# A four-layer graph network on one core: the products of layer 0 a batch later, four rows' sums ahead of the last two, and later small steps in layer 1

## The chip, the cores and the metric

The kernel runs on one core of a Trainium2 chip. The metric is device time in microseconds (us) of the whole kernel. The core has five engines that issue their instructions in order, each on its own: TensorE (PE, matmuls and transpositions), VectorE (DVE), ScalarE (ACT), GpSimd (POOL) and SyncE (SP, which here starts most DMA transfers). Matmuls accumulate in PSUM[...]; the rest is in SBUF, and large matrices are in DRAM.

## The reference

A graph has N = 3125 nodes with 128 features, and 103,125 edges: 50,000 random pairs in both directions, and a loop on each node. Four layers follow each other.

```python
# layer 0: weighted sum over the edges, bias, relu; then layer norm of x + out
xw  = x @ weight
out = relu(segment_sum(edge_weight[:, None] * xw[src], dst) + b)
# layer 1: attention with 4 heads of 32
e     = leaky_relu(a_s[src] + a_d[dst])
p     = exp(e - segment_max(e, dst)[dst])
alpha = p / (segment_sum(p, dst)[dst] + 1e-16)
out   = segment_sum(h[src] * alpha[:, :, None], dst) + gat_bias + x @ skip_W + skip_b
# then a layer norm of its own, and another one around x + out
# layer 2: attention with Q, K, V over the same edges, softmax per receiver
# layer 3: two products with the mean over the neighbours (w1_l, w1_r, b1, w2_l, w2_r, b2)
```

## The kernel before, in words

The nodes make 25 blocks of 128. Sums over edges are done as matmuls with dense block matrices. Two of these are built first, in DRAM: `wd`, the summed weights of the edges between each two blocks, and `ctd` (`f_ctd` in the trace), their counts.

**Edge stage** (from L841). The edges, sorted, are cut into windows; 40 batches of 16 windows. For a batch DVE makes two one-hot masks (`ohd`, `ohc`, L865) and their products with the weights in three bf16 parts (`wod`, L876; the last part in halves with ACT, L882). `make(b + 1)` runs while PE works on batch b. For each four windows PE does 8 matmuls `cp` (counts, L911) and 24 `wp` (weights, L919), and ACT copies both out of PSUM (`cs` L924, `ws` L930). SP stores `ws` to `wd` after each batch (L941), and `cs` to `ctd` after each second one.

**Layer 0** runs inside that. Row i of `wd` is complete some batches before the end. Then `adds0` issues on SP the loads of the row's 20 blocks (two tiles `cw` of 640 KB, pool `f_zp` of four buffers) and puts 20 products (L820, two passes each) on the list `todo`. After each four windows up to three of the list are issued on PE. The program writes the order of PE and SP out by hand in this stage (`manual_schedule`); on DVE and ACT a scheduler orders.

```python
            if order:
                m = min(3, len(todo)) if b > 3 else 0
                for f in todo[:m]:
                    f()
                del todo[:m]
                if len(todo) <= 20 and (done + 1) * P <= (b - 1) * BW * WN:
                    todo += adds0(zp, done, acc0, (0, Z0))
                    done += 1
```

The sums for blocks 0 to 19 (`acc0`) take five PSUM banks, so blocks 20 to 24 (`acc1`) can't be summed in the same stage. After the last batch comes the **tail**: what is left of `todo`, and the last rows of `acc0`. Then `front.close()` frees the memory of the edge stage, and the **left rows** follow: all 25 rows once more for blocks 20 to 24, five products a row, loads of 320 KB in a pool of eight buffers (`f_tp1`). Beside them run the end of layer 0 (`end0`: relu, add, layer norm; `r` L832), the attention scores of layer 1 (`scores1`, `top`, `factors`), hung on rows by `marks`, and `values`, which makes layer 1's `vp` for two blocks at a time.

**Layer 1** loops over items (g, hp, c): four groups g of 6, 7, 6 and 6 destination blocks, two pairs of heads hp, and 25 source blocks c. A half pass is one (g, hp). `masks` loads counts (`ct1`) and makes a mask `cm` for each head, two of five in one DVE instruction (L1280), the others on ACT (`fm` L1286) and DVE (L1287). `products` does three matmuls a block (L1297, L1302 twice). At c = 24 `sums` adds up on DVE (`nz` L1321), and POOL and DVE divide. Small work is put between the items: `later(k, f)` hands f to the k-th `step()` from now, and there is one step an item. After a group's second half `finish1` runs: norm, scale, multiply and add on POOL, norm, scale, and then `turns`: the blocks of the group one by one are transposed (L1044), multiplied (L1048) and copied to `vo` (L1050, `self__8043` in the trace), in the one or two PSUM banks that `few` gives (two only where the group has under seven blocks). `skips` (L1310, L1311) starts the next group's sum for the residual.

**Layer 2** loops over two halves q of the destination blocks (13 and 12) and 25 source blocks c: scores L1445 on PE, exponential L1448 on ACT, counts L1449 on DVE, products L1453. `degrees` prepares the division of layer 3 (`rt` L1425). **Layer 3** is two passes (L1553, L1629).

## Time and profile before

| | |
|---|---|
| median of 3 runs | 1505.42 us (1503.63 to 1510.78) |
| the profiled execution | 1509.73 us |
| its span, as the profile has it | 1507.9 us |
| PE busy, PEld (weight loads) busy | 1394.0, 1225.2 us |
| DVE, ACT, POOL busy | 981.9, 908.5, 129.5 us |
| mean granted clock of PE | 0.974 |
| edges end (last wp) | 463.3 us |
| last product of blocks 0 to 19 | 488.6 us |
| left rows | 494.5 to 537.2 us |
| half passes of layer 1 start their `nz` at | 596.4, 638.7, 699.0, 749.9, 806.4, 851.6, 905.3, 946.2 us |

The profile is that of one execution. Its page cuts the span in 40 slices and gives for each the busy share of every engine in tenths, the granted clock of PE (PEclk) in tenths of full speed, and the share of the DMA engines. A row of PE's timeline has start, length, engine, line, operation, output and inputs by the program's names, and in brackets the idle time just before it and what ended that. A row of the chain of waits has start, length and what took it. Half passes are cut here at the start of `nz`: what PE does in 638.7 to 699.0 is the half pass (1, 0), and so on.

### The profile page before, as it was taken

The numbers are of one execution on the slowest core, as the hardware profiler recorded it, in microseconds if no ns is written. First come the engines' busy times: TensorE is split into PE (matmuls) and PEld (weight loads), VectorE is DVE, ScalarE is ACT, GpSimd is POOL, SyncE is SP. The second block draws the span as 40 slices with busy tenths as digits, with TensorE's granted clock in tenths as the row PEclk, the third lists the DMA queues.
The fourth block names the chain that finished last, engine by engine and source line by source line (L and its number), as shares of the span: only waits on it lengthen the run. The fifth ranks groups of instructions, "written<-read, shape, count | busy, mean of one in ns | idle before, by whom it ended". The sixth has DMA issues, their size and how long they took to land.

```text
span 1507.9 us, 35015 instructions
## 1 busy us (share of the span) xinstructions
PE 1394.0 (92%) x14762; PEld 1225.2 (81%) x14775; DVE 981.9 (65%) x1621; ACT 908.5 (60%) x1857; POOL 129.5 (9%) x164
## 2 busy tenths in 40 slices
PE   3889999999998988988979989899999999999995
PEld 3889999999998877987978989677777774458995
DVE  4989899999991389887888879544464351012006
ACT  2978789888882489877777787454465331023003
POOL 1000000000000023132032113200000000000000
PEclk8999999999999999999999999999999999999998
DMA  7378788989887733433534534332222218513641
GB/s 206 94 184 229 194 221 241 236 212 229 240 213 223 230 115 114 138 106 107 142 83 116 143 86 116 124 112 69 69 64 77 81 58 299 198 43 131 199 154 46
DMA packets 209732, 223.91 MB, mean 148 GB/s; under 512 B 72988, under 2 KB 183371, under 8 KB 209309
## 3 DMA queue, kind: packets, MB, share of 16 engines
q1 hardware_dynamic: 208780, 218.51, 50.5%
q8 instruction: 117, 1.92, 0.5%
q0 software_dynamic: 400, 1.97, 0.4%
q10 hardware_dynamic: 385, 1.11, 0.2%
q14 instruction: 50, 0.41, 0.1%
HBM read 157.19 MB, written 64.36 MB: 147 GB/s over the span
## 4 chain that ended last, share of the span: by engine, by line
PE 72%; DVE 10%; ACT 8%; DMA 5%; issue 3%; POOL 2%; SPq 0%; DVEq 0%; ACTq 0%; POOLq 0%
PE wp L919 11%; PE acc L1453 9%; PE acc L1302 9%; PE s L1445 8%; PE acc L1553 7%; PE acc L1629 6%; PE acc L820 6%; PE acc L1297 5%; PE cp L911 4%; DVE cm L1287 3%; ACT wod L882 3%; DMA cw<-wd 2%; PE left L820 2%; ACT fm L1286 1%; DVE cm L1280 1%
## 5 line engine op out<-in xcount | busy, mean ns | idle before, releaser
L1302 PE MATMUL acc<-vp,cm 128*128 128x198 bf16 x2500 | 343.3, 252 | 7.6 <-DVE cm L1287 6.5
L1297 PE MATMUL acc<-vp,ct 128*128 128x204 bf16 x1250 | 316.5, 255 | 10.2 <-DVE vp L1205 4.5
L1286 ACT ACTIVATE fm<-adr,bas 128x768 bf16<-128x768 f32 (+1 forms) x320 | 287.2, 952 | 62.2 <-DVE cm L1287 60.4
L1302 PEld LDWEIGHTS <-cm 128*128 128x128 bf16 x2500 | 235.7, 98 | 24.4 <-DVE cm L1287 8.8
L919 PE MATMUL wp<-wod,ohc 128*128 128x128 bf16 x3768 | 239.1, 220 | 6.8 <-ACT cs L924 5.0
L919 PEld LDWEIGHTS <-ohc 128*128 128x128 bf16 x3768 | 220.3, 98 | 8.3 <-issue 7.8
L876 DVE TENSOR_TENSOR wod<-ohd,w 128x4096 bf16<-128x4096 bf16 (+2 forms) x122 | 221.5, 1869 | 0.4 <-PE wp L919 0.4
L1287 DVE TENSOR_TENSOR cm<-fm,ct 128x768 bf16<-128x768 bf16 (+1 forms) x320 | 200.3, 657 | 32.1 <-PE acc L1302 16.3
L882 ACT ACTIVATE wod<-ohd,wu 128x128 bf16<-128x128 bf16 x628 | 197.9, 398 | 0.0
L1449 DVE TENSOR_TENSOR e<-e,ct 128x416 f32<-128x416 f32 (+1 forms) x175 | 108.1, 624 | 110.2 <-ACT e L1448 102.1
L1448 ACT ACTIVATE e<-s,f_nm 128x416 f32<-128x416 f32 (+1 forms) x175 | 109.5, 632 | 103.1 <-PE s L1445 95.5
L1453 PEld LDWEIGHTS acc<-self__8043,e 128*128 128x128 f32 x1250 | 148.2, 193 | 19.8 <-issue 18.9
L820 PE MATMUL acc<-f_xw,cw 128*128 128x128 f32 x1000 | 146.8, 288 | 11.1 <-DMA cw<-wd 11.1
L1453 PE MATMUL acc<-self__8043,e 128*128 128x129 f32 x1250 | 148.5, 276 | 0.0
L1445 PE MATMUL s<-yT,f_xT 128*128 128x416 f32 (+1 forms) x350 | 143.1, 545 | 4.5 <-ACT rt L1425 2.5
L820 PEld LDWEIGHTS acc<-f_xw,cw 128*128 128x128 f32 x1000 | 126.5, 196 | 11.8 <-DMA cw<-wd 11.8
L1297 PEld LDWEIGHTS <-ct 128*128 128x128 bf16 x1250 | 121.8, 98 | 4.1 <-issue 2.9
L924 ACT CAST cs<-cp 128x500 bf16<-128x500 f32 x157 | 90.6, 577 | 39.1 <-PE cp L911 39.1
L1445 PEld LDWEIGHTS s<-yT,f_xT 128*128 128x128 f32 x350 | 62.6, 192 | 55.3 <-issue 40.8
L865 DVE TENSOR_TENSOR ohd<-kd,ramp 128x4096 bf16<-128x4096 bf16 (+1 forms) x41 | 90.2, 2201 | 20.2 <-PE cp L911 18.3
L930 ACT COPY ws<-wp 128x512 f32<-128x512 f32 x157 | 90.1, 578 | 20.6 <-PE wp L919 20.3
L911 PE MATMUL cp<-ohc,ohd 128*128 128x125 bf16 x1256 | 96.0, 220 | 4.1 <-ACT ws L930 3.8
(345 smaller groups left out, 1526.3 us busy)
## 6 DMA issues: line engine op xcount, KB each, us to landing
ct<-f_ctd SPq DMA_DIRECT2D x46, 800.0 KB
wd<-ws SPq DMA_DIRECT2D x39, 896.0 KB
cw<-wd SPq DMA_DIRECT2D x50, 640.0 KB
ct<-f_ctd SPq DMA_DIRECT2D x150, 192.0 KB
f_ctd<-cs SPq DMA_DIRECT2D x20, 1000.0 KB
ct<-f_ctd SPq DMA_DIRECT2D x50, 224.0 KB
ct<-f_ctd SPq DMA_DIRECT2D x25, 416.0 KB
ct<-f_ctd SPq DMA_DIRECT2D x25, 365.2 KB
```

Source lines behind the costliest of these rows:

```text
L820: steps.append(lambda j=j, a=cw[:, j - h, :]: nc.tensor.matmul(accs[j // 4][:, j % 4, :], a, xw[:, i, :], start=False, stop=(i == NB - 1 a ...
L876: tip[s] = nc.vector.tensor_tensor(packed(f, ww), packed(ohd, ww), twos(w2[s])[:, ww], OP.mult)
L882: nc.scalar.activation(wod[2][:, BW + w, :], ohd[:, BW + w, :], AF.Copy, scale=w3[:, 1, at : at + 1])
L911: nc.tensor.matmul(cp[:, j, 0:KW], ohd[:, w, :], ohc[:, w, 0:KW], start=(j == 0 and q == 0), stop=(j == 3 and q == 1), skip_group_check=True,)
L919: made = nc.tensor.matmul(wp[:, j, :], ohc[:, w, :], wod[s][:, w, :], start=(j == 0 and q == 0 and s == 0), stop=(j == 3 and q == 1 and s ...
L1286: nc.scalar.activation(f[:, : n * P], at, AF.Relu, bias=bas[:, c, h : h + 1], scale=UP)
L1287: nc.vector.tensor_tensor(m[:, : n * P], f[:, : n * P], ct[:, : n * P], OP.min)
L1297: nc.tensor.matmul(out_(F1, PW), ct[:, k * P : (k + 1) * P], vp[:, c, hp : hp + 2, :, 2 * F1 : V1], start=(c == 0), stop=False, skip_group ...
L1302: nc.tensor.matmul(out_(0, 2 * F1)[:, j], ms[j][:, k * P : (k + 1) * P], vp[:, c, hp + j, :, 0 : 2 * F1], start=False, stop=(c == NB - 1 a ...
L1445: nc.tensor.matmul(s[:, :m], xT[:, c * P : (c + 1) * P], yT[:, i0 * P + a : i0 * P + a + m], start=True, stop=True)
L1448: nc.scalar.activation(e[:, a : a + m], s[:, :m], AF.Exp, bias=nm[:, q : q + 1], scale=scale)
L1453: nc.tensor.matmul(acc[k // 3][:, (k % 3) * (P + 1) : (k % 3 + 1) * (P + 1)], es[q, c][:, k * P : (k + 1) * P], vo[:, c, 0 : P + 1], start ...
```

## The change

It has these parts:

- The products from `todo` start at batch 5 instead of 4: twelve of them move behind the last batch.
- After the last batch the three PSUM banks of the edge stage are closed at once (`three`), and the banks of blocks 20 to 24 are opened in the tail with their bias. After row 22 come rows 0 to 3 for blocks 20 to 24 (ZA = 4), in the same four buffers, and then rows 23 and 24 for blocks 0 to 19. By the order of the program row 22's loads, which were issued in the last but one batch, now stand in the tail behind the last stores.
- The pools for counts (`f_cp1`) and for one factor of the masks (`f_dp1`) are opened ahead of the pool of the left rows, so in memory of their own; the pool of the masks stays in the memory of the left rows.
- The left loop starts at row 4. Its marks move on by four rows; `values` stand after rows 16, 18, 19, 21, 22 and 24 instead of every odd row from 13.
- The masks of the first two items are emitted ahead of `end0` of blocks 20 to 24.
- `norm1` loses its square root, which becomes a step of its own (`root`), a gap later; `finish1`'s gaps go from (1, 5) to (2, 9), for the last group from (1, 1) to (1, 2); `turns` start four steps after the second scale instead of one; `bound2` of the first half waits three steps, and three more.
- `skips` start at c = 5 instead of 2, and `degrees` at c = 16 instead of 3; `finish2` has the root as a step too.

```diff
@@ -495,6 +495,7 @@
 NBT = NW // BW
 LW = 4
 NL = (NBT - 1) * BW + LW
+ZA = 4
 Z0 = 20
 V1 = 100
 GA = 80.0
@@ -570,7 +571,8 @@
     op_ = front.enter_context(tc.tile_pool(name="f_oh", bufs=2))
     of_ = front.enter_context(tc.tile_pool(name="f_of", bufs=6))
     ep = front.enter_context(tc.tile_pool(name="f_ep", bufs=1))
-    cps = front.enter_context(tc.tile_pool(name="f_cps", bufs=3, space=PSUM))
+    three = ctx.enter_context(ExitStack())
+    cps = three.enter_context(tc.tile_pool(name="f_cps", bufs=3, space=PSUM))
     ramp = ep.tile([P, P], BF16, name="ramp")
     thr = ep.tile([P, NG], F32, name="thr")
     row_i = ep.tile([P, NG], I32, name="row_i")
@@ -929,7 +931,7 @@
                 cur[3](k)
             nc.scalar.copy(ws[:, k : k + 4, :], wp)
             if order:
-                m = min(3, len(todo)) if b > 3 else 0
+                m = min(3, len(todo)) if b > 4 else 0
                 for f in todo[:m]:
                     f()
                 del todo[:m]
@@ -955,9 +957,21 @@
             order = ExitStack()
             order.enter_context(tc.manual_schedule(engines={mybir.EngineType.PE, mybir.EngineType.SP}))
     order.close()
+    three.close()
+    zpp = zero.enter_context(tc.tile_pool(name="f_zpp", bufs=1, space=PSUM))
+    left = GB[Z0 // 4 :]
+    acc1 = [zpp.tile([P, 4, P], F32, name=f"left{k}") for k in range(len(left))]
+    t8 = zpp.tile([P, 512], F32, name="tr_sa")
+    for a, (b0, n) in zip(acc1, left):
+        bias0(a, n)
     for f in todo:
         f()
-    for i in range(done, NB):
+
+    for i in range(done, NB - 2):
+        add0(zp, i, acc0, (0, Z0))
+    for i in range(ZA):
+        add0(zp, i, acc1, (Z0, NB - Z0))
+    for i in range(max(done, NB - 2), NB):
         add0(zp, i, acc0, (0, Z0))
     front.close()
     r = xw
@@ -1023,8 +1037,10 @@
             nc.vector.bn_aggr(mv[:, b, :], bs[:, b, :])
         sd = sp.tile([P, 13], F32, name="sd1")[:, 0:n]
         nc.vector.tensor_scalar(sd, mv[:, :, 1], EPS, None, OP.add)
-        nc.scalar.activation(sd, sd, AF.Sqrt)
         return sp, mv, sd
+
+    def root(state):
+        nc.scalar.activation(state[2], state[2], AF.Sqrt)
     def norm2(state, o, i, i0, n):
         sp, mv, sd = state
@@ -1056,15 +1072,22 @@
         i0, n = QG[q]
         mq = sp.tile([P, 1], F32, name="mq")
         nc.vector.tensor_reduce(mq, nq[:, i0 : i0 + n], AX.X, OP.max)
-        d = highest(sp, mq, 1)
-
-        def rest():
+        wait = 1 if q else 3
+
+        def rest(d):
             mm = sp.tile([P, 1], F32, name="mm")
             spread(d, 1, mm)
             nc.scalar.activation(mm, mm, AF.Sqrt)
             nc.vector.tensor_scalar(nm[:, q : q + 1], mm, -1.0001, None, OP.mult)
-        later(1, rest)
+        def over():
+            d = highest(sp, mq, 1)
+            later(wait, lambda: rest(d))
+
+        if q:
+            over()
+        else:
+            later(wait, over)
     def finish1(sp, g, gap):
@@ -1075,7 +1098,8 @@
         def first_norm():
             keep["a"] = norm1(sp, r, i0, n)
-            later(gap[0], first_scale)
+            later(gap[0], lambda: root(keep["a"]))
+            later(gap[0] + 1, first_scale)
         def first_scale():
             norm2(keep["a"], r, r, i0, n)
@@ -1086,12 +1110,13 @@
         def second_norm():
             keep["b"] = norm1(sp, r, i0, n)
-            later(gap[0], second_scale)
+            later(gap[0], lambda: root(keep["b"]))
+            later(gap[0] + 1, second_scale)
         def second_scale():
             norm2(keep["b"], x, r, i0, n)
             nc.gpsimd.memset(vo[:, i0 : i0 + n, P : P + 1], 1.0)
-            later(gap[0], lambda: turns(0))
+            later(1 if g == len(IG) - 1 else 4, lambda: turns(0))
         def turns(j):
             if j < n:
@@ -1126,14 +1151,10 @@
         HW = 3 * PW
         fp = st.enter_context(tc.tile_pool(name="f_fp1", bufs=2))
+        cp = st.enter_context(tc.tile_pool(name="f_cp1", bufs=6))
+        dp = st.enter_context(tc.tile_pool(name="f_dp1", bufs=2))
         tail = ExitStack()
         tp = tail.enter_context(tc.tile_pool(name="f_tp1", bufs=8))
-        zpp = zero.enter_context(tc.tile_pool(name="f_zpp", bufs=1, space=PSUM))
-        left = GB[Z0 // 4 :]
-        acc1 = [zpp.tile([P, 4, P], F32, name=f"left{k}") for k in range(len(left))]
-        t8 = zpp.tile([P, 512], F32, name="tr_sa")
-        for a, (b0, n) in zip(acc1, left):
-            bias0(a, n)
         for g in range(Z0 // 4):
             end0(acc0[g], *GB[g])
@@ -1207,7 +1228,7 @@
                 )
         spare.append(lambda: zps.tile([P, 512], F32, name="few", tag="acc1"))
-        marks = {3: lambda: scores1(0), 4: lambda: (scores1(1), scores1(2)), 5: lambda: scores1(3), 6: lambda: scores1(4)}
+        marks = {7: lambda: scores1(0), 8: lambda: (scores1(1), scores1(2)), 9: lambda: scores1(3), 10: lambda: scores1(4)}
         keep = {}
         def top():
@@ -1216,23 +1237,19 @@
             nc.vector.tensor_reduce(ex, sa[:, 0:Z0, 0:H].rearrange("p b h -> p h b"), AX.X, OP.max)
             keep["d"] = highest(fp, ex, H)
-        marks[7] = top
-        marks[9] = lambda: (spread(keep["d"], H, km), factors(0, Z0))
+        marks[11] = top
+        marks[13] = lambda: (spread(keep["d"], H, km), factors(0, Z0))
         ready = 0
-        for i in range(NB):
+        for i in range(ZA, NB):
             add0(tp, i, acc1, (Z0, NB - Z0))
             if i in marks:
                 marks[i]()
-            if i >= 13 and i % 2:
+            if i >= 16 and i % 3 != 2:
                 values(ready)
                 ready += 2
         tail.close()
-        cp = st.enter_context(tc.tile_pool(name="f_cp1", bufs=6))
         mp = st.enter_context(tc.tile_pool(name="f_mp1", bufs=8))
-        dp = st.enter_context(tc.tile_pool(name="f_dp1", bufs=2))
         sp = st.enter_context(tc.tile_pool(name="f_sp1", bufs=2))
-        for g, (b0, n) in enumerate(left):
-            end0(acc1[g], b0, n)
         later(3, lambda: scores1(Z0 // 4))
         later(5, lambda: scores1(Z0 // 4 + 1))
         later(7, lambda: factors(Z0, NB - Z0))
@@ -1342,12 +1359,16 @@
                 rh = r[:, i0 : i0 + n, hp * C : (hp + 2) * C].rearrange("p b (h c) -> p b h c", c=C)
                 nc.gpsimd.tensor_tensor(rh, rh, hi[:, :, :, 0:C], OP.add)
                 if hp == H - 2:
-                    later(1 if last else 3, lambda: finish1(ends[-1], g, (1, 1) if last else (1, 5)))
+                    later(1 if last else 3, lambda: finish1(ends[-1], g, (1, 2) if last else (2, 9)))
             later(1 if last else 4 if g else 7, quotients)
         ends.append(sp)
         acc = None
+        for y_ in range(2):
+            masks(*items[y_])
+        for g, (b0, n) in enumerate(left):
+            end0(acc1[g], b0, n)
         for x_, (g, hp, c) in enumerate(items):
             i0, n = IG[g]
             if (g, hp, c) == (1, 0, 0):
@@ -1367,7 +1388,7 @@
                     acc += [zpp.tile([P, 512], F32, name="acc1", tag=k) for k in ("tr_sa", "left0", "left1")]
                 else:
                     acc = [ap.tile([P, 512], F32, name=f"acc1_{k}") for k in range(n)]
-            if c == (2 if g else 0) and hp == (0 if g else H - 2):
+            if c == (5 if g else 0) and hp == (0 if g else H - 2):
                 later(0, lambda: skips(i0, i0 + n))
             if (g, hp, c) == (0, 2, 5):
                 later(0, in_range)
@@ -1375,7 +1396,7 @@
             if g == 0 and hp == 0 and ready < NB and ready <= c + 4:
                 values(ready)
                 ready += 2
-            for y_ in range(x_ if x_ == 0 else x_ + 2, min(x_ + 3, len(items))):
+            for y_ in range(x_ + 2, min(x_ + 3, len(items))):
                 masks(*items[y_])
             if c < NB - 2:
                 for k in range(n):
@@ -1464,7 +1485,8 @@
             def one(h):
                 keep[h] = norm1(ends[-1], r, *halves[h])
-                later(1, lambda: two(h))
+                later(1, lambda: root(keep[h]))
+                later(2, lambda: two(h))
             def two(h):
                 norm2(keep[h], x, r, *halves[h])
@@ -1488,7 +1510,7 @@
             if c == 0:
                 acc = [ap.tile([P, 512], F32, name=f"acc2_{k}") for k in range((n + 2) // 3)]
             step()
-            if (q, c) == (0, 3):
+            if (q, c) == (0, 16):
                 degrees()
             if (q, c) == (1, 12):
                 for b in range(2):
```

## The prediction

> **What bounds the kernel now.** I read the page's slices first, then the times by stage, then TensorE's (PE's) own gaps, and for each long gap the chain of work.
>
> ```profile
> PE   3889999999998988988979989899999999999995
> DVE  4989899999991389887888879544464351012006
> PEclk8999999999999999999999999999999999999998
> DMA  7378788989887733433534534332222218513641
> ```
>
> A slice is 37.7 us. PE is busy nearly throughout (92% of the span), so a gain must come out of its gaps, or out of time in which it works slowly. In the first twelve slices VectorE (DVE) is as busy as PE, and the DMA engines are mostly at .7 to .9.
>
> ```profile
> core 0: us, PE busy (x) PEld busy (x) DVE busy (x) ACT busy (x) POOL busy (x), PEclk, DMA share, GB/s
> 146.00:160.00 14.00, 12.82 (x141) 12.59 (x142) 7.95 (x5) 8.05 (x22) 0.00 (x0) 0.76 0.68 230
> 463.30:488.60 25.30, 20.92 (x173) 20.53 (x170) 3.70 (x23) 2.32 (x4) 1.45 (x2) 0.93 0.77 239
> 494.60:537.20 42.60, 42.57 (x333) 38.68 (x333) 18.92 (x62) 19.57 (x40) 7.04 (x22) 0.96 0.60 194
> 638.70:749.90 111.20, 101.16 (x1080) 96.97 (x1079) 91.22 (x164) 85.48 (x112) 25.01 (x18) 0.98 0.43 121
> 749.90:851.60 101.70, 88.96 (x941) 85.00 (x940) 86.08 (x174) 77.11 (x115) 24.46 (x18) 0.97 0.39 112
> 851.60:946.20 94.60, 87.79 (x929) 84.42 (x927) 78.26 (x158) 70.05 (x103) 25.00 (x18) 0.96 0.37 103
> ```
>
> The rows are: a piece of the edge stage after a stall, the tail (edges' end to the last product of blocks 0 to 19), the left rows, and three stretches of layer 1, each two half passes long. PE idles 10.0, 12.7 and 6.8 us in those three. PE's timeline says for whom (in brackets the idle time before an instruction, and what ended it):
>
> ```profile
> 107.78 0.49 PE L820 MATMUL acc<-f_xw,cw 128*128 128x128 f32 x2 [3.54 <-DMA cw<-wd]
> ...
> 147.16 1.22 PE L820 MATMUL acc<-f_xw,cw 128*128 128x128 f32 x4 [2.94 <-DMA cw<-wd]
> ...
> 477.90 1.43 PE L820 MATMUL acc<-f_xw,cw 128*128 128x128 f32 x5 [4.34 <-DMA cw<-wd]
> ...
> 689.26 0.47 PE L1044 MATMUL few<-f_ident,f_x 128*128 128x128 f32 x1 [2.51 <-DVE self__8043 L1050]
> ...
> 711.00 0.33 PE L1044 MATMUL few<-f_ident,f_x 128*128 128x128 f32 x1 [2.31 <-DVE self__8043 L1050]
> ...
> 780.38 0.26 PE L1302 MATMUL acc<-vp,cm 128*128 128x198 bf16 x1 [1.76 <-DVE cm L1287]
> ...
> 787.91 0.48 PE L1044 MATMUL acc<-f_ident,f_x 128*128 128x128 f32 x1 [5.95 <-ACT f_x L1035]
> ...
> 882.83 0.26 PE L1302 MATMUL acc<-vp,cm 128*128 128x198 bf16 x1 [3.17 <-DVE cm L1287]
> ...
> 979.26 1.02 PE L1445 MATMUL s<-yT,f_xT 128*128 128x416 f32 x1 [2.54 <-ACT rt L1425]
> ```
>
> Three are layer 0's products waiting for a load, five are layer 1's finish of a group, the last is `degrees`. They cost more than their length. After most of them the granted clock falls to half for 3.4 or 6.8 us, half of which is lost: 3.4 after 107.78, 6.8 about 147.16 (.76 in the row above), 3.4 about 477.90, 3.4 about 689.26, 6.8 about 787.91 and about 882.83, 3.4 about 979.26.
>
> **Edge stage: products from batch 5.** Four windows cost PE 0.44 + 1.34 + 0.72 = 2.50 us (chain: cp, wp, six passes of products), 10.0 a batch. The load of row 1 landed 7.16 us after its issue, that of row 3 10.62:
>
> ```profile
> 100.58 7.16 DMA cw<-wd
> ...
> 136.50 10.62 DMA cw<-wd
> ```
>
> With a batch more of lead a row is used 16.7 us or more after its issue, so I let both stalls and a small third one (0.25 at 235.47) go: 6.7, with (3.4 + 6.8)/2 = 5.1 of slow clock, and 2.9 for twelve products that leave batch 4: 14.7 for PE. DVE can't follow so far.
>
> ```profile
> L876 DVE TENSOR_TENSOR wod<-ohd,w 128x4096 bf16<-128x4096 bf16 (+2 forms) x122 | 221.5, 1869 | 0.4 <-PE wp L919 0.4
> L865 DVE TENSOR_TENSOR ohd<-kd,ramp 128x4096 bf16<-128x4096 bf16 (+1 forms) x41 | 90.2, 2201 | 20.2 <-PE cp L911 18.3
> ```
>
> Two masks of 2.20 and three products (mean 1.87, the full ones 2.2) make 9.9 us a batch. DVE idled 3.13 (108.82), 1.61 (120.46) and 6.05 (156.57) because PE was late, 10.8 in all; beyond that it sets the pace. **-11** (bounds -9 and -13).
>
> **Tail.** Two things get worse. Twelve products stand behind the edges' end, 12 x 0.226 = 2.7 (40 passes took 4.52). And row 22's load, which was issued before the last stores, is now queued on SP behind the stores of wd and of the counts f_ctd, as its buffers come free only in the tail. Counted from the edges' end (463.3): issue at 7.0, landed at 14.56 by the 7.55 that the load from 470.31 took, while PE has work until 7.45: a stall of 7.1 where 4.34 was. Row 22 is done at 20.7, the four moved rows for blocks 20 to 24 (4 x 5 x 0.226 = 4.5) at 25.3. Row 23 takes the buffers of those rows, freed at 22.0; with some 3.4 us for a load here (the tail's last rows moved at 410 GB/s, and a row is 1.28 MB) it is there at 25.4, just not late. Rows 23 and 24 take 9.0: end at 34.45, where before has 25.25. **+9.2** (bounds +5, if row 22 comes as quickly as a load does on a free queue, and +14, if rows 23 and 24 take 7 to 10 us each).
>
> [...] half clock followed the 2.94 (6.8 us) and the 2.54 (3.4). I go by the rows: small stalls are worth 1.7 to 3.4 more when they go[...], and the tail loses about what it loses now, with 1.7 in its upper bound.
>
> **Left rows and the switch.** The left loop has four rows fewer, -4.5; PE is full there (42.57 of 42.60), so all of it counts. The six `values` are spread over rows 16 to 24 instead of 13 to 23: PE's number of them is the same, DVE's 2.7 us each fits in 9 rows of 1.1 us and other work. From 537.2 to 543.2 PE worked 0.96 of 6.0: it waited 2.78 for counts ct, 1.27 for `r` (end0), 1.02 for the first mask. The counts now have memory of their own and are loaded early, and the first masks stand ahead of end0. The masks' own memory is still under the left rows' loads, so ACT and DVE start only after the last product: I take 3.3 us to the first product, **-2** net (0 to -4).
>
> **Layer 1.** The Sqrt that ACT ran straight behind DVE's statistics now comes a step or two later (an item takes 1.6 to 2.2 us of PE). ACT issues in order, so until now its masks stood behind a Sqrt that waited for some 2 us of bn_stats; that is 780.38 and 882.83 (PE waits for cm, cm for ACT). The first transposition of a group is put off 4 items, over 6.5 us, more than the 5.95 that it waited for norm2. Gains: stretch 638.7: 2.51 + 2.31 + 0.8 (the skips, now at c = 5) + 1.7 of clock = 7.3. Stretch 749.9: 1.76 + 5.95 + 3.4 of clock = 11.1; but DVE is busy 86.1 of 101.7 and I leave it 6.6 of slack: 9. Stretch 851.6: 3.17 + 3.4 of clock = 6.6, less 1.6, since the last group keeps short gaps: 5. Sum **-21** (bounds -10, if half of the stalls only move, and -30, all of PE's idle time). Added waits: behind a later Sqrt stand ACT's masks as before, but its operand is then ready. Put off are norm2, POOL's three passes of 2.3 us each, the transpositions (now in the next group's second half) and bound2; layer 2, from 953 on, needs none of them at once: the last group's blocks, put off by some 3 items, are the last six of its first pass; if they come late, +2.
>
> **Layer 2.** `degrees` goes from c = 3 to c = 16: 2.54 + 1.7 = 4.2 could go; as its copy rt still stands on ACT between the exponentials of the scores, **-3.5** (0 to -4.2). finish2's root adds one step each, free inside other work, up to +1.
>
> **Sum.** -11 + 9.2 - 4.5 - 2 - 21 - 3.5 = -32.8. The profiled execution took 1509.73 (span 1507.9 and 1.8 around it), 4.3 above the median of the runs, 1505.42: 1476.9 for an execution like that, 1472.6 against the median. I say 1472.
>
> **Rivals.**
> - Stalls move. Layer 1's PE, DVE and ACT are all at 75 to 90%; what is taken from one wait turns up in the next, and layer 1 gains 8 instead of 21; with half of the switch and of degrees gone too, 1472 + 13 + 2 = 1488. For it: DVE 86.1 of 101.7. Against: PE's waits there are few and long, not many and short.
> - The tail costs more: row 22, 23 and 24 each wait for a load of 7 to 10 us in the chain of four buffers, another +9 and 1.7 of clock: 1483. For it: 7.55 in this very place. Against: the stores are over by then.
> - The edges gain little, since DMA (221 to 241 GB/s in these slices) makes the loads as late as the products: -3 instead of -11: 1480.
> - Slower: the transpositions of 19 blocks (6 + 7 + 6) move into the second half of the next group, right where DVE also divides (nz, rz) and makes masks, and with 7 blocks they share one bank. If each waits for DVE's copy of the one before, as at 711.00, that is 19 x 2.31 = 44 us; with the rest, -33 + 44 = +11: 1516. It ends above 1512.9 from 2.1 us a block, (33 + 7.5)/19. For it: two such waits are there now. Against: two turns are two items apart, 3.4 us or more, and in the present stretch only two of the blocks waited.
> - The new order doesn't happen, because a buffer still holds it: 1500. In the changed program the order of instructions does move as described; this is small.
>
> **Chances.** The forecast .55 (its own range 1464 to 1480); stalls move .17; tail .11; edges .08; slower .05; no effect .04. Range 1460 to 1493: it takes in the first three rivals. What a measurement here can tell from no change is about 0.5%, 7.5 us: faster below 1497.9, slower above 1512.9: .91, .05, .04.
>
> **What would show it.** No PE gap for cw between 100 and 240, clock 1.0 there, and the edges end at about 452. A stall of 7 us for row 22 about 460, none of over 1 us for rows 23 and 24. The first cm product some 3 us after the last left one. No wait of over 2 us for cm, x or the one bank in layer 1, and none for rt in layer 2. Wrong it would be if a second stall stands in the tail, if the edges' DVE idles as much as before, or if layer 1's halves keep their lengths of 50 to 60 us.

## The result, and the profile after

The changed kernel took 1515.64 us (median of 5 runs, 1514.23 to 1516.95), the kernel before 1508.13 beside it: ratio 1.0054, interval 1.0038 to 1.0069. It is slower by about 8 us, where the sum of the prediction had 33 faster. Span against span it is 1513.8 to 1507.9.

The times by stage (the columns as in the prediction's table) are cut where the changed kernel's stages end: edge stage to and from batch 10, tail, left rows, then the three pairs of half passes of layer 1.

```profile
core 0: us, PE busy (x) PEld busy (x) DVE busy (x) ACT busy (x) POOL busy (x), PEclk, DMA share, GB/s
107.00:147.00 40.00, 39.32 (x589) 38.98 (x587) 40.00 (x21) 34.64 (x98) 0.00 (x0) 1.00 0.90 239
147.00:464.20 317.20, 302.27 (x4464) 298.38 (x4462) 286.33 (x173) 259.26 (x718) 1.35 (x1) 0.98 0.83 215
464.20:501.40 37.20, 27.95 (x226) 27.19 (x225) 3.69 (x23) 2.32 (x4) 1.45 (x2) 0.91 0.70 217
501.40:541.90 40.50, 39.36 (x305) 34.02 (x306) 19.42 (x78) 21.14 (x47) 5.96 (x17) 1.00 0.74 240
644.70:758.20 113.50, 102.46 (x1078) 98.99 (x1076) 92.26 (x165) 86.15 (x112) 25.34 (x18) 0.95 0.41 118
758.20:856.70 98.50, 90.85 (x944) 86.36 (x942) 86.23 (x175) 76.98 (x115) 25.50 (x18) 0.97 0.41 117
856.70:950.30 93.60, 86.39 (x929) 82.30 (x927) 78.83 (x159) 70.02 (x103) 23.76 (x18) 1.00 0.38 103
```

The first row is what I had forecast: no stall, full clock. The second gives it all back: from batch 10 to the edges' end it takes 317.2 us where the kernel before takes 304.4, and 15 us of it are PE's idle time. The layer 1 rows are 2.3 us longer, 3.2 and 1.0 shorter than before. PE's gaps of over 2 us behind 107, all twelve, by its timeline:

```profile
154.99 0.33 PE L921 MATMUL wp<-wod,ohc 128*128 128x128 bf16 x3 [2.22 <-ACT ws L932]
...
242.97 0.72 PE L921 MATMUL wp<-wod,ohc 128*128 128x128 bf16 x10 [3.07 <-ACT ws L932]
...
330.22 0.48 PE L921 MATMUL wp<-wod,ohc 128*128 128x128 bf16 x3 [2.68 <-ACT cs L926]
...
479.04 0.58 PE L822 MATMUL acc<-f_xw,cw 128*128 128x128 f32 x1 [7.46 <-DMA cw<-wd]
...
546.76 0.42 PE L1319 MATMUL acc<-vp,cm 128*128 128x198 bf16 x3 [4.10 <-DVE cm L1297]
...
663.09 0.38 PE L1327 MATMUL few<-f_l_swt,f_xT 128*128 128x128 f32 x1 [3.89 <-DVE f_xw L1328]
...
706.18 0.33 PE L1314 MATMUL acc<-vp,ct 128*128 128x204 bf16 x1 [3.92 <-DVE nz L1338]
...
792.27 0.26 PE L1319 MATMUL acc<-vp,cm 128*128 128x198 bf16 x1 [2.29 <-DVE cm L1297]
...
812.30 0.25 PE L1314 MATMUL acc<-vp,ct 128*128 128x204 bf16 x1 [2.10 <-DVE nz L1338]
...
886.80 0.26 PE L1319 MATMUL acc<-vp,cm 128*128 128x198 bf16 x1 [2.12 <-DVE cm L1304]
...
916.74 0.48 PE L1064 MATMUL acc<-wyv,f_xT 128*128 128x256 f32 x1 [2.05 <-DVE f_xT L540]
...
986.14 1.06 PE L1466 MATMUL s<-yT,f_xT 128*128 128x416 f32 x1 [3.85 <-ACT e L1469]
```

The stalls that I had named are gone (cw in the edge stage, the transpositions of 2.5, 2.3 and 5.95 us); others of the same size stand a few us beside them. The difference of 5.9 us by the two traces, stage by stage (the edges' end is the end of the last wp here, 463.5 for the 463.3 given above):

| stage | before | after | change | forecast |
|---|---|---|---|---|
| edges' end | 463.5 | 464.2 | +0.7 | -11 |
| tail | 25.1 | 37.2 | +12.1 | +9.2 |
| left rows with what starts them | 48.6 | 40.5 | -8.1 | -4.5 |
| left rows' end to the first `nz` | 59.2 | 60.7 | +1.5 | -2 |
| first `nz` to the last half pass's | 349.8 | 347.7 | -2.1 | -21 |
| from there to layer 3 | 293.7 | 296.0 | +2.3 | -3.5 |
| layer 3 | 268.0 | 267.5 | -0.5 | 0 |

### The profile page after: what moved, and what is told of

The parts are those of the page before. It is cut to its first block, busy times and chain, and to the rows that moved or that the text cites. A ratio compares the mean times of both kernels' runs of the same rounds, so it can differ in the third digit from the quotient of the medians.

```text
span 1513.8 us, 35038 instructions
## 1 busy us (share of the span) xinstructions
PE 1396.5 (92%) x14775; PEld 1225.5 (81%) x14775; DVE 982.7 (65%) x1621; ACT 908.3 (60%) x1857; POOL 131.4 (9%) x164
## 3 DMA queue, kind: packets, MB, share of 16 engines
q8 instruction: 117, 1.92, 0.5%
q10 hardware_dynamic: 385, 1.11, 0.2%
## 4 chain that ended last, share of the span: by engine, by line
PE 72%; DVE 12%; ACT 8%; DMA 3%; issue 3%; POOL 2%; ACTq 0%; DVEq 0%; POOLq 0%
PE wp L921 10%; PE acc L1319 9%; PE acc L1474 9%; PE s L1466 8%; PE acc L1575 7%; PE acc L1651 6%; PE acc L822 6%; PE acc L1314 5%; ACT wod L884 4%; PE cp L913 3%; DVE cm L1304 3%; PE left L822 1%; DMA cw<-wd 1%; DVE cm L1297 1%; DVE nz L1338 1%
## 5 line engine op out<-in xcount | busy, mean ns | idle before, releaser
L1319 PE MATMUL acc<-vp,cm 128*128 128x198 bf16 x2500 | 346.9, 252 | 13.0 <-DVE cm L1297 6.4
L1314 PE MATMUL acc<-vp,ct 128*128 128x204 bf16 x1250 | 317.2, 256 | 12.8 <-DVE nz L1338 8.0
L1304 DVE TENSOR_TENSOR cm<-fm,ct 128x768 bf16<-128x768 bf16 (+1 forms) x320 | 204.2, 666 | 32.0 <-PE acc L1319 15.6
L932 ACT COPY ws<-wp 128x512 f32<-128x512 f32 x157 | 89.8, 578 | 11.9 <-PE wp L921 11.9
```

What stands on the lines that cost most here:

```text
L1304: nc.vector.tensor_tensor(m[:, : n * P], f[:, : n * P], ct[:, : n * P], OP.min)
L1314: nc.tensor.matmul(out_(F1, PW), ct[:, k * P : (k + 1) * P], vp[:, c, hp : hp + 2, :, 2 * F1 : V1], start=(c == 0), stop=False, skip_group ...
L1319: nc.tensor.matmul(out_(0, 2 * F1)[:, j], ms[j][:, k * P : (k + 1) * P], vp[:, c, hp + j, :, 0 : 2 * F1], start=False, stop=(c == NB - 1 a ...
```

## The experiments

Each kernel's median stands beside that of the kernel before in the same series; the ratio is to that.

| kernel | us | before | ratio, interval | edges end | last `nz` starts |
|---|---|---|---|---|---|
| the kernel before, its own trace | | 1508.13 | 1 | 463.5 | 948.8 |
| the change | 1515.64 | 1508.13 | 1.0054 (1.0038 to 1.0069) | 464.2 | 952.9 |
| edges_only | 1513.52 | 1507.68 | 1.0045 (1.0032 to 1.0058) | 461.8 | 952.4 |
| ws_first | 1511.45 | 1507.68 | 1.0034 (1.0021 to 1.0047) | 457.2 | 950.1 |
| steps_only | 1506.59 | 1507.68 | 0.9999 (0.9988 to 1.0010) | 460.7 | 946.7 |
| bn_later | 1499.74 | 1507.68 | 0.9948 (0.9938 to 0.9958) | 464.9 | 944.5 |
| row22_first | 1511.97 | 1507.05 | 1.0044 (1.0030 to 1.0057) | 461.7 | 947.4 |
| ws_own | 1510.25 | 1507.05 | 1.0022 (1.0011 to 1.0033) | 457.9 | 949.0 |
| values_old | 1514.05 | 1507.05 | 1.0044 (1.0023 to 1.0064) | 462.0 | 952.2 |
| before_bn | 1501.31 | 1507.05 | 0.9961 (0.9951 to 0.9971) | 461.2 | 944.9 |
| bn_skips | 1500.87 | 1506.19 | 0.9953 (0.9933 to 0.9973) | 461.9 | 944.5 |
| all_fixed | 1493.51 | 1506.19 | 0.9921 (0.9905 to 0.9938) | 457.8 | 933.1 |
| all_fixed_za0 | 1489.58 | 1506.19 | 0.9894 (0.9877 to 0.9910) | 458.8 | 932.3 |
| steps_bn | 1492.35 | 1506.19 | 0.9904 (0.9887 to 0.9920) | 461.1 | 936.5 |
| split_only | 1513.94 | 1506.75 | 1.0052 (1.0033 to 1.0071) | 462.0 | 951.9 |
| split_all | 1485.06 | 1506.75 | 0.9854 (0.9834 to 0.9874) | 458.9 | 929.0 |
| act_order | 1477.01 | 1505.80 | 0.9808 (0.9783 to 0.9832) | 451.5 | 920.1 |
| act_order_b4 | 1475.44 | 1505.80 | 0.9795 (0.9769 to 0.9821) | 452.7 | 918.4 |

The last two columns are read from one trace each; the same code's edges ended between 461.7 and 464.9 in seven of them, so a difference of 3 us there means nothing by itself. By the time alone edges_only, ws_first, row22_first, values_old and split_only are not told apart from the change: their intervals overlap its own. What they show is in their traces.

### The edge stage

ScalarE's timeline about PE's wait of 3.07, first in the changed kernel, then at the same batch in the kernel before:

```profile
239.39 0.71 ACT L708 CAST w<-wu 128x256 bf16<-128x256 f32 x2 [1.11 <-DVE wu L707]
240.01 2.44 ACT L884 ACTIVATE wod<-ohd,wu 128x128 bf16<-128x128 bf16 x8
242.35 1.05 ACT L932 COPY ws<-wp 128x512 f32<-128x512 f32 x2
```

```profile
247.59 2.44 ACT L882 ACTIVATE wod<-ohd,wu 128x128 bf16<-128x128 bf16 x8
249.94 0.56 ACT L930 COPY ws<-wp 128x512 f32<-128x512 f32 x1
```

In the changed kernel two copies ws stand behind eight mask products wod for the next batch, in the other one. Nothing in the change touches ScalarE in this stage: moving products on PE made the scheduler order ScalarE anew. DVE's order is the same in both but for two small instructions (wt and wu about 327) that changed places with a wod.

**edges_only**

```diff
-                m = min(3, len(todo)) if b > 3 else 0
+                m = min(3, len(todo)) if b > 4 else 0
```

> The kernel before with the products from batch 5, nothing else. Theory A (ScalarE's order): in the changed kernel the 12 us won by batch 10 were lost again at later batches because the scheduler, given the new start, puts ScalarE's mask products (wod) for the next batch ahead of the copies ws that free PSUM. The same order stands here, so the edges end within 1.5 us of 463.3 again (batch 10 about 12 us earlier, batch 27 level), and with the later load of row 22 and twelve products more in the tail (some 6 us) the time is 1512 to 1516. Theory B (other parts of the change disturb the edge stage): edges end at about 452, time about 1503.

Measured: batch 10 11.3 us earlier, edges' end 461.8, waits for ws of 2.2 and 3.1 and for cs of 2.7 at the same batches as in the change; 5.8 us slower. So no other part of the change disturbs the stage.

**ws_first and ws_own**

```diff
             if cur and (b + 1 < NBT - 1 or k < LW):
-                cur[3](k)
-            nc.scalar.copy(ws[:, k : k + 4, :], wp)
+                with tc.issue_after(copied.ins) if copied else ExitStack():
+                    cur[3](k)
+            copied = nc.scalar.copy(ws[:, k : k + 4, :], wp)
```

In ws_own the copy comes first, and cur[3](k) is held behind it.

> The changed kernel, with each quarter batch's wod on ScalarE held behind the copy ws of the quarter before; no work added or removed. Theory A (ScalarE's order gives the gain back): PE's waits for ws of 2.2 to 3.1 us about 155, 243 and 330 go, the edges end at 452 to 457, time 1504 to 1509. Theory C (VectorE's 9.9 us a batch and the key batches hold the stage anyway): the waits only change their name, edges end at 461 or later, time 1512 to 1516.

> The changed kernel, with each quarter batch's wod on ScalarE behind the copy ws of the same quarter (ws_first held it behind that of the quarter before, and won back 7 of the 12 us). Theory A (ScalarE's order): the rest of PE's waits for cs and ws shrinks too, edges end at 450 to 455, 1 to 4 us faster than ws_first's 1511.5. Theory C (VectorE's key batches hold the rest): edges end at 455 to 458, within 1 us of ws_first or up to 3 slower.

Measured: the edges end 7.0 and 6.3 us earlier than in the change, but the batches from the tenth on still take 10.6 us each on average. In ws_own the largest wait for a copy is 1.04; in ws_first 2.24 (155), 2.02 (241) and 1.21 (325) are left of the three that were to go. Theory A has its sign, not its whole size: both end later than I expected (457.2 for 452 to 457, 457.9 for 450 to 455), and ws_first's time lies between the two theories.

**dve_less and keys_less**, each all_fixed_za0 with one thing left out:

```diff
+            if s == 1:
+                wod.append(wod[0])
+                continue
```

```diff
-        kd2, kc2, w2, w3 = keys[b // 8]
+        kd2, kc2, w2, w3 = keys[min(b // 8, 1)]
```

(keys_less also drops the calls that prepare keys in the loop.)

> all_fixed_za0 with the second of the three weight parts left out on VectorE (the first part is used twice, so the weights are wrong): 2.2 us a batch less for VectorE, the same work for PE. If VectorE holds the edge stage: the loss per eight batches of some 4 us falls to under 1, edges end at 440 to 445. If the key batches hold it by their chain over ScalarE and PSUM: edges end at 450 or later.

> all_fixed_za0 without the preparation of keys from batch 16 on (the second group's keys are used again, so the matrices are wrong). If the key batches hold the edge stage: batches take 10.0 to 10.1 from batch 12 on, edges end at 441 to 446. If VectorE's steady 9.9 us does: 0.8 lost in each second batch stays, edges end at 449 to 453.

Measured, one execution each: the edges end at 457.1 and 457.9, for 458.8 in all_fixed_za0. Neither holds the stage. In dve_less DVE is busy 224 of 309 us, and the batches keep their lengths to 0.4 us:

```profile
148.00:457.00 309.00, 297.98 (x4460) 293.67 (x4459) 224.19 (x142) 258.92 (x719) 1.35 (x1) 1.00 0.85 221
```

In keys_less the long key batches go, and every other batch then takes 10.8 and 10.4 instead of 10.0. (Its total, 6820.75, is no time of this path: with the wrong matrices the kernel goes on into its general path.) ScalarE's timeline there shows why:

```profile
341.93 0.58 ACT L922 CAST cs<-cp 128x500 bf16<-128x500 f32 x1 [1.45 <-PE cp L909]
344.44 0.58 ACT L922 CAST cs<-cp 128x500 bf16<-128x500 f32 x1 [1.93 <-PE cp L909]
344.91 0.59 ACT L926 COPY ws<-wp 128x512 f32<-128x512 f32 x1
```

ScalarE idles for copies cs that aren't ready while a finished ws (its products ended at 343.23) waits behind them until 344.91. It is the order again, of cs against ws this time.

**act_order and act_order_b4**: split_all (below) with cs held too, then with the later start taken back.

```diff
-            nc.scalar.copy(
-                cs[:, :, i0 : i0 + 4 * WN].rearrange("p c (w i) -> p c w i", i=WN),
...
+            with tc.issue_after(copied.ins) if copied else ExitStack():
+                nc.scalar.copy(
+                    cs[:, :, i0 : i0 + 4 * WN].rearrange("p c (w i) -> p c w i", i=WN),
...
```

> split_all with each copy cs on ScalarE held behind the ws of the quarter before as well (so cs, ws, wod in turn), no work changed. If the rest of the edge stage's loss is ScalarE's order: edges end at 444 to 450, PE's waits of 0.66 for cs go, time 1475 to 1481. If it is something else: edges end at 454 or later, 1483 to 1488.

> act_order with the products from batch 4 again, as in the kernel before. If the later start is worth the two stalls once ScalarE's order is held (the term of 11 in my prediction, less the 2.7 and some that the tail pays): 5 to 10 us slower than act_order. If the later start brings nothing even then: within 3 us of act_order.

Measured: the edges end 7.4 us earlier than in split_all (a little later than the 444 to 450 expected), the time 8 us shorter, as expected; most batches take 10.0 us, PE's own time. And the later start wins nothing as it stands. Without it, in act_order_b4, the two stalls for cw are back (2.38 and 1.92 us) and the stage ends 1.2 us later, but the tail is 2.1 shorter (25.3 against 27.4); the median is 1.6 us lower, within the intervals. One batch of act_order, the 27th, still takes 16.5 us where act_order_b4 takes 11.6: casts of the keys, which I did not hold, stand ahead of a ws there and wait for VectorE (PE waits 2.79 us for that ws):

```profile
320.37 0.40 ACT L708 CAST w<-wu 128x256 bf16<-128x256 f32 x1 [1.89 <-DVE wu L707]
320.68 0.58 ACT L932 COPY ws<-wp 128x512 f32<-128x512 f32 x1
```

With those 4.9 us repaired the later start might be worth some 3 us (an estimate, 4.9 less the 1.6 between the medians); that was not run. The order costs the old start too: from batch 10 to the edges' end act_order_b4 takes 298.7 us, the kernel before 304.4. So of what act_order wins, a part had been lost in the kernel before as well.

### Layer 1 and layer 2

**steps_only**: the kernel before with root, gaps, turns, skips, bound2, degrees and finish2 as in the change.

> The kernel before with only the small steps of layers 1 and 2 of the change (root, gaps, turns, skips at c = 5, bound2, degrees at c = 16). My prediction's steps: -24, about 1484. Theory D (the second norm's statistics keep their place in VectorE's order, behind masks of item 64, 115 and 164 in both kernels, and wait for GpSimd's three passes in both): layer 1 gains 0 to 4, layer 2 loses 1 or so, time 1504 to 1510.

Measured: 1506.59, no change. The forecast of -24 fails on its own, without the other parts. Why is to be seen where PE waits for cm at 792.27. GpSimd's timeline, then VectorE's, of the changed kernel:

```profile
783.16 2.32 POOL L1106 TENSOR_TENSOR f_xw<-f_xw,f_g_row 128x896 f32<-128x896 f32 x1 [10.37 <-ACT f_xw L1051]
785.56 2.28 POOL L1107 TENSOR_TENSOR f_xw<-f_xw,f_b_row 128x896 f32<-128x896 f32 x1
787.92 2.28 POOL L1108 TENSOR_TENSOR f_xw<-f_xw,f_x 128x896 f32<-128x896 f32 x1
```

```profile
783.88 4.38 DVE L1304 TENSOR_TENSOR cm<-fm,ct 128x768 bf16<-128x768 bf16 x2 [0.34 <-ACT fm L1303]
790.23 1.07 DVE L1035 BATCH_NORM_STATS2 bs<-f_xw 128x6 f32<-128x128 f32 x5 [1.97 <-POOL f_xw L1108]
791.22 1.00 DVE L1297 SCALAR_TENSOR_TENSOR cm<-adr,nas,ct 128x768 bf16<-128x768 f32 x1
```

The second norm's statistics (BATCH_NORM_STATS2) stand in VectorE's order ahead of masks that are ready, and wait for the third pass. Counted in items, they stand behind the masks of item 63, 115 and 164 in the kernel before and 64, 115 and 164 in the change. The gap that went from 5 to 9 moved the call in the program, not the instruction. In layer 2 the same wait is 5.52 us in both kernels; ScalarE's Sqrt waits 4.61 for it, and the exponentials behind it.

**bn_later and before_bn**: the change, and the kernel before, with the statistics held in place (made_ is the last mask, or the last product with counts in layer 2).

```diff
-            keep["b"] = norm1(sp, r, i0, n)
+            with tc.issue_after(made_[0].ins):
+                keep["b"] = norm1(sp, r, i0, n)
```

> The changed kernel, with the second norm's statistics on VectorE held behind the masks that stand ahead of them in the program (so at item 74, 121 and 171 instead of 64, 115 and 164; in layer 2 behind the scores emitted so far). Theory D (statistics that wait for GpSimd hold up the masks behind them): the waits of VectorE for f_xw (1.7, 2.0, 3.6, 5.5 us) go, and PE's of 2.3, 2.1 and 3.9 with part of the half clock: 8 us faster than the changed kernel, about 1507. Theory E (layer 1 is full, stalls move): within 2 us of the changed kernel, 1513 to 1516.

> The kernel before with the second norm's statistics on VectorE held behind the masks ahead of them in the program. With its gap of 5 that moves them only from item 63, 115 and 164 to 68, 115 and 165. Theory D (it is the place in VectorE's order, and the longer gap of the change only helps once the place is held): the stalls at 780 and 883 stay, the first group's and layer 2's go, time 1500 to 1505. If the hold alone were worth what it brought on the changed kernel (16 us): 1492.

Measured: bn_later is 16 us faster than the change, twice what I expected. Times by stage of bn_later, for the same three pairs of half passes:

```profile
648.40:756.00 107.60, 98.60 (x1078) 95.72 (x1076) 93.13 (x164) 86.05 (x112) 26.86 (x18) 1.00 0.43 125
756.00:850.70 94.70, 87.73 (x943) 83.79 (x941) 87.33 (x174) 76.74 (x115) 25.50 (x18) 1.00 0.42 122
850.70:941.90 91.20, 85.79 (x929) 82.51 (x928) 81.71 (x159) 70.18 (x103) 23.95 (x18) 1.00 0.38 106
```

12.1 of it come in layer 1 (293.5 for 305.6), with the clock full throughout; the wait of 3.85 and its 6.8 us of half clock in layer 2 go too. PE's waits for cm of 2.29 and 2.12 shrink to 1.09 and 1.49, and a new one of 3.56 for f_xT comes (717.74). With the old gap of 5 the hold moves the statistics only to item 68, 115 and 165: of the waits for cm one stays (1.75 for 1.76) and one shrinks (1.82 for 3.17), layer 2's goes, 5.7 us gained. So the hold and the longer gaps need each other: the small steps alone win nothing (steps_only), the hold alone 5.7, and both together, in steps_bn below, 14 (steps_bn also has its skips at c = 13, which bn_skips shows to be worth nothing).

**bn_skips** (bn_later with `skips` at c = 13 instead of 5):

> bn_later with the skips of a group at c = 13 instead of 5. Theory I (at c = 5 the skips' adds stand on VectorE behind the first norm's statistics, in one PSUM bank, and PE waits 3.8, 1.3 and 1.0): those waits go, 3 to 6 us faster than bn_later's 1499.7, so 1494 to 1497. Theory E (layer 1 is full, the stall moves): 1498 to 1501.

Measured: no gain. The waits of 3.79, 1.31 and 1.04 became 2.02, 2.32 and 2.05, and one of 1.50 for cm came. I had the place of the skips wrong as a cause: at c = 13 they meet GpSimd's passes instead of the first norm (split_all, below, bears this out).

**split_only and split_all**: the change, and all_fixed_za0, with GpSimd's three passes cut by block.

```diff
-            nc.gpsimd.tensor_tensor(rs, rs, g_row[:, None, :].to_broadcast([P, n, P]), OP.mult)
...
+            for b in range(n):
+                nc.gpsimd.tensor_tensor(rs[:, b, :], rs[:, b, :], g_row, OP.mult)
+                nc.gpsimd.tensor_tensor(rs[:, b, :], rs[:, b, :], b_row, OP.add)
+                nc.gpsimd.tensor_tensor(rs[:, b, :], rs[:, b, :], xs[:, b, :], OP.add)
```

> The changed kernel with GpSimd's three passes of finish1 cut into pieces of one block (3 x n instead of 3), nothing else. Theory K (a mask operation of VectorE with two inputs that meets a GpSimd pass is held until the pass ends): masks beside GpSimd fall from up to 2.6 us to under 1, PE's waits for cm of 2.3 and 2.1 shrink to 1 or less, time 1505 to 1511. Theory D alone (VectorE only waits for the end of the third pass): the waits for f_xw stay or, with dearer small passes, grow; time 1514 to 1518.

> all_fixed_za0 (1489.6) with the passes cut into pieces of one block. Theory K: the waits of 2.0 to 2.3 for the skips and 3.55 for a transposition, which stand behind masks held by GpSimd, go: 1480 to 1486. Otherwise 1488 to 1493.

Measured: split_only gains nothing. The statistics of each block now wait for its piece (three times running 0.94 us), and PE waits 3.18 for cm. Where the statistics are held, split_all gains 4.5 us, and the three waits for the skips are gone; the one of 3.55 for a transposition, which was to go too, stays. What VectorE's masks lose beside GpSimd hardly falls in sum (33.9 to 30.9 us in layer 1): it comes in smaller portions, 1.89 us for the longest mask instead of 2.43, and GpSimd itself now takes 58.7 us for the pieces where the passes took 24.1. So both things cost, and cutting the passes helps only once the place of the statistics is set.

### The tail, the left rows, and the sum

**row22_first**

```diff
+        if b == NBT - 1:
+            todo += adds0(zp, done, acc0, (0, Z0))
+            done += 1
         if b % SB == SB - 1:
```

> The changed kernel, with row 22's two loads put on SP ahead of the last store of the counts f_ctd. Theory F (the tail's stall of 7.46 is row 22's load standing behind f_ctd, 1 MB in 320-byte packets): the stall falls to 3 to 4 us, time 1511 to 1513. Rival G (the load is held by the buffers of row 20 or slow wherever it stands): stall 6 or more, time 1514 to 1517.

Measured by PE's timeline, the stall falls as theory F has it; a wait for a moved row's tile (`left`) comes, for which the prediction had nothing. The time falls by 1.5 us by the two ratios, within their intervals:

```profile
472.11 0.38 PE L822 MATMUL acc<-f_xw,cw 128*128 128x128 f32 x1 [2.99 <-DMA cw<-wd]
...
478.92 0.38 PE L822 MATMUL left<-f_xw,cw 128*128 128x128 f32 x1 [2.08 <-DMA cw<-wd]
```

**values_old**

```diff
-            if i >= 16 and i % 3 != 2:
+            if i >= 13 and i % 2:
```

> The changed kernel, with the six values after the odd rows 13 to 23 as before. Theory H (the first mask of layer 1 stands on VectorE behind the values that were pushed into the last nine rows): PE's waits at the start of layer 1, 4.10 and 1.11, fall to about 1 to 2 together, time 1511 to 1514. Rival (the masks' memory, still under the left rows' loads, or the factors hold them, or PE then waits in the left rows): 1514 to 1517.

Measured: the two waits fall only to 3.27 and 0.86, and the time hardly moves. The rows on which the six `values` stand are not the point: the factors they need come 67 us behind the edges' end in either case (fa at 531.6 in the change, at 529.0 here), and VectorE idles 6.0 us for the scores just before.

**all_fixed, all_fixed_za0 and steps_bn.** all_fixed has ws_own, row22_first, bn_later and skips at c = 13; all_fixed_za0 has ZA = 0 and marks and values as before; steps_bn is steps_only with the hold and those skips.

> The changed kernel with four repairs: wod behind ws of its quarter, row 22's load ahead of f_ctd, second norm's statistics held back, skips at c = 13. If the causes found are separate, the gains add: 5 + 4 + 16 + 4, time 1484 to 1490. If they overlap or new waits come, above 1491.

> all_fixed without the four moved rows (ZA = 0, marks and values as before). Theory J (the moved rows only take cover away: the left rows hide the scores, factors and values that layer 1 needs, and four rows fewer show again as the waits of 4.1 and 1.1 at layer 1's start): equal or up to 5 us faster than all_fixed. My prediction's step (the moved rows fill the wait for row 23, and -2 at the switch): 2 to 5 us slower.

> The kernel before with the small steps of the change, the second norm's statistics held back and skips at c = 13; edges, tail and left rows as before. Theory D: layer 1 and 2 gain as in bn_later and bn_skips, from a start 6 us earlier than in the changed kernel: 1488 to 1493. If the hold needs the rest of the change: 1498 or more.

Measured: all_fixed is 1.33% of the time ahead of the change (by the two ratios), 20 us where the parts expected added up to 29; the skips brought nothing, and the edge repair and the hold overlap or fall short by the rest. Without the moved rows it is 3.9 us faster (the intervals just overlap): PE's waits at layer 1's start, 4.24 and 1.11 in all_fixed, become 1.82 and 0.92, and the first `nz` comes 2.2 us earlier though the edges end 1.0 later in that trace. steps_bn is about as fast as these, with the whole first half of the change left out.

## Why the prediction was wrong, point by point

Two terms carried 32 of the 33 us, the edge stage and layer 1. Both failed for the same kind of reason: the order of an engine other than PE (ScalarE in the edge stage, VectorE in layer 1), which the prediction took as given.

- **Edge stage** (-11, measured +0.7). The stalls and the slow clock went as I said, and batch 10 came 11.9 us earlier, about what I had taken from VectorE's idle time. The failed step is "beyond that it sets the pace": VectorE doesn't (dve_less). One of its three idle times, 1.61 at 120.46, had been ended by ScalarE, and I read it as PE's:

```profile
120.46 2.29 DVE L865 TENSOR_TENSOR ohd<-kd,ramp 128x4096 bf16<-128x4096 bf16 x1 [1.61 <-ACT wod L882]
```

  I treated the order on ScalarE as given. It was made anew by the scheduler, and its copies came later behind mask products or unready copies, at 155, 243, 330 and in many batches besides. That this order is the cause is shown by ws_first and act_order, which hold it and change no work: 7 and then 7 us more of the edges' end, part of which the old order had cost too. The rival that I gave this outcome, DMA loads as late as the products, named the wrong cause: after 107 no product in the edge stage waited for a load.
- **Tail** (+9.2, measured +12.1). The mechanism held: row 22 behind f_ctd, 7.46 for 7.1. Row 23, which the sum had as just not late, came 1.64 us late, and the clock was at half for 6.8 us from 476.
- **Left rows and switch** (-6.5, measured -6.6 together). That the sum fits is luck: two errors cancel. The four rows counted fully, and the left stage was 3.6 us shorter beyond them: 1.5 of it an earlier start after the tail, and some 1.8 the half clock that the kernel before had in its left rows until 498.06 (0.96 there, 1.00 in the change), which I had counted as full work. But the switch lost 1.5 instead of winning 2. I had counted `values` as fitting into the last nine rows. The four rows were cover for the chain of scores, factors and `values`, of which `values`, 17 us of VectorE, can only start with the factors. From the factors to the end of the left rows there were 14.1 us before and 10.3 after, and what no longer fits stands in front of layer 1's first mask. all_fixed_za0 against all_fixed bears this out; values_old shows that rearranging the values alone doesn't help.
- **Layer 1** (-21, measured -2.1). The step "ACT's masks stood behind a Sqrt that waited for bn_stats; that is 780.38 and 882.83" is wrong. In the kernel before these two Sqrts started at 785.25 and 884.88, when PE had its masks already. At 780.38 the mask came late because VectorE made it beside GpSimd's passes (it and the one ahead of it took 4.14 us together, where the median alone is 0.55 each), at 882.83 because it stood behind statistics that waited for GpSimd:

```profile
775.47 2.09 POOL L1082 TENSOR_TENSOR f_xw<-f_xw,f_g_row 128x896 f32<-128x896 f32 x1 [10.50 <-ACT f_xw L1035]
777.64 2.27 POOL L1083 TENSOR_TENSOR f_xw<-f_xw,f_b_row 128x896 f32<-128x896 f32 x1
776.19 4.14 DVE L1287 TENSOR_TENSOR cm<-fm,ct 128x768 bf16<-128x768 bf16 x2 [1.24 <-ACT fm L1286]
785.25 0.21 ACT L1026 ACTIVATE sd<-sd 128x7 f32<-128x7 f32 x1 [3.96 <-DVE sd L1025]
...
881.25 1.07 DVE L1021 BATCH_NORM_STATS2 bs<-f_xw 128x6 f32<-128x128 f32 x5 [3.58 <-POOL f_xw L1084]
```

  The change moves neither the statistics nor the passes away from the masks. The transpositions' waits (10.8 us by the rows) did go. But the skips' wait grew from 2.31 to 3.89, and waits for `nz` at the ends of half passes came (3.92, 2.10): PE's idle time in the three stretches fell only from 29.6 to 25.9 us, and half clock was 17 us in both kernels. Of the rival "stalls move" this is the stronger form, but layer 1 was not full, which was my argument for it: bn_later takes 12 us out of it.

  At 706.18 VectorE had idled 4.80 us for counts ct, whose loads stood on SP behind the load of adr (issued 696.60), which waits for the last masks of the half pass before. That wait is in the kernel before too (688.66), hidden then by PE's own stall. No run isolates it.
- **Layer 2** (-3.5, measured +2.3). The row said that PE waited for rt, and I took `degrees` for the cause. rt was only the last in ScalarE's queue, behind the Sqrt that waited for VectorE's statistics, and these for GpSimd. Moved to c = 16, `degrees` ran at 1063 without a stall, and the wait stayed, 3.85 for 2.54, until bn_later held the statistics.
- **The slower rival** (a chain of 19 transpositions, each waiting for the copy to `vo`) did not occur: the one such wait of any size is 0.71 us (722.82); two more in these turns, 1.21 (719.57) and 2.05 (916.74), are for the copy of the transposed block itself. The time is on the slower side for another reason, the order of ScalarE and VectorE, which I had not listed.

What stays open: the wait at 706.18 by itself, and how the 5.8 us of edges_only divide between edge stage and tail, since single traces of the same edge code differ by 3 us.

## What to carry to other kernels

Where a scheduler orders an engine, a shift on one engine reorders others: compare the orders of every engine in the stage, not only of those the diff names, before you count a gain. A wait's named releaser is the last in a queue; follow the queue back to the first instruction in it that isn't ready, and ask whether the change moves that one. Work that is moved out of a stage also takes away the cover of what ran beside it. The best kernel here (act_order_b4, 2.05% faster than before, interval 1.79 to 2.31) keeps of the change only the small steps (skips at c = 13), the early memory for counts and the early first masks. It leaves both moves of layer 0's products out, puts row 22's load ahead of the counts' store, cuts GpSimd's passes, and holds two engines to an order.

## What the runs showed of the hardware

- VectorE's mask operation with two bf16 inputs in SBUF (cm, L1304) took 0.55 us alone (median of 248) and 1.06 beside a GpSimd instruction (median of 72, up to 2.44, about the length of one pass of 2.3). Above, two masks take 4.38 us beside two passes. The five longest, 2.02 to 2.44, each started while a pass ran and ended 0.42 to 0.49 after that pass: the one of 2.44 ended at 788.26, its pass at 787.84. Over layer 1 the masks take 33 us more of VectorE's time than alone.
- The clock fell to half about stalls of 2.22, 3.07, 2.68, 2.29 and 2.10 us (from 155.40, 244.15, 329.48, 793.69 and 814.17), 3.4 us each time, but not about 2.12 (886.80). These starts lie 88.75, 85.33, 464.21 and 20.48 us apart, which is 26, 25, 136 and 6 steps of 3.413 us (464.21 / 136). In the step ahead of the five falls PE worked 1.19, 1.18, 1.47, 1.21 and 1.69 us. Stretches of the changed kernel, a step each (columns as above): the stall at 154.99 leaves PE 1.19 us of work in one step, and the next is at half clock; the one at 886.80 lies across two steps and leaves 2.24 and 2.19, at full clock; but after a step with 1.53, from 913.16, the clock stayed full too (1.00 in 916.57 to 919.98), so what decides it stays open.

```profile
151.99:155.40 3.41, 1.19 (x19) 1.05 (x19) 3.41 (x5) 2.82 (x9) 0.00 (x0) 1.00 1.11 259
155.40:158.81 3.41, 3.41 (x29) 3.35 (x27) 1.15 (x4) 3.30 (x10) 0.00 (x0) 0.50 0.85 165
882.44:885.85 3.41, 2.24 (x26) 2.00 (x23) 0.24 (x2) 1.33 (x2) 3.05 (x2) 1.00 0.49 128
885.85:889.26 3.41, 2.19 (x19) 1.62 (x19) 3.41 (x13) 1.76 (x2) 0.00 (x0) 1.00 0.13 44
913.16:916.57 3.41, 1.53 (x18) 1.30 (x15) 3.41 (x8) 2.16 (x4) 1.23 (x1) 1.00 0.46 120
```
